# Feature parts kept once in DRAM and loaded in three runs, and the source row spread for plain quads alone

## The chip, the cores and the metric

The kernel runs on one core of a Trainium2 chip. The metric is the device time of one execution in microseconds; runs of the same kernel here lie within about 0.2% of each other (2110.19 to 2114.73 us for the kernel before). Engine names follow the profile: PE is TensorE's matmul, PEld its weight load, DVE is VectorE, ACT is ScalarE, POOL is GpSimd and SP is SyncE, which here only issues DMAs.

## The reference

One layer of a graph network with 6250 nodes, 128 features and 200,000 edges. The edges come sorted by `dst`; `src` is random.

```python
h   = maximum(layernorm(x), 0)
xw  = h @ W_in                                        # one row of 128 per node
W_e = (ssp(f_e @ W_f1 + b_f1) @ W_f2 + b_f2) * c_e    # f_e: 20 features of an edge, c_e: its weight
out = segment_sum(xw[dst_e] * W_e, src_e)             # gather by dst, add up by src
y   = x + ssp(out @ W_o1 + b_o1) @ W_o2 + b_o2        # ssp(v) = softplus(v) - log 2
```

## The kernel before, in words

**Units of work.** The edges are cut into chunks of 128, quads of 512 (four chunks; 391 of them) and super chunks of 1024 (two quads; 196). The main loop has one iteration per quad, and the order of every instruction is written out by hand: iteration `i` runs one stage of quad `i`, the next stage of quad `i-1`, and so on, and calls hooked functions at named points (`"L"`, `"D0"`, `"PE2"`, `"D2"`, ...). The order of recording is the order on each engine.

**What a quad passes through.** `s1_pe` (L290) multiplies the features by `W_f1` on PE; ACT computes Abs, Exp, Ln (L295 to L301); DVE adds up the softplus (L325). `s2_pe_x` (L340) picks the rows of `xw` by a one-hot matrix, `s2_pe_w` (L348) multiplies by `W_f2`, ACT scales (L353) and DVE multiplies (L358). What follows differs:

- A *plain* quad (237 of them) compares its sources with each other: `s1_eq` (L319) sets a row of 512 sources, spread over all 128 partitions in the tile `sb`, against the column of sources. `s3_pe` (L370) adds equal sources up, `s3_copy` (L378, ACT) copies the sums to the tile `s` (five buffers), `s3_ji` (L399, ACT) makes the row numbers, and `s3_scatter` issues four scatters (L418), one per chunk.
- A *permuted* quad (154 of them, list `mpq`: quads 8, 10, 13, 15, 18, ... to 390) is sorted by permutation matrices (L528, L621) into `accT` in SBUF. `s1_eq`, `s3_copy` and `s3_scatter` return at once for it, so it never reads `sb`. Two of them share one scatter of overflow rows: 77 in all.

**Scatters.** A scatter is an indirect DMA with add that POOL issues into one of four accumulators in DRAM. Two into the same accumulator may not overlap, so each waits for the one before it in its accumulator. `acc_of` picks the accumulator by the scatter's number `k`: 0 for the first two, then `k % 2` up to 8, `k % 3` up to 140 and `k % 4` after that. POOL's queue does almost nothing else from 48.8 us to 2048 us.

**Features.** A matmul in bf16 keeps fp32 accuracy here by splitting: `fb_1` to `fb_4` cut a block of 4096 edges' features into three bf16 parts (`f3[:, 0]`, `[:, 1]`, `[:, 2]`). The contraction has 6 x 20 = 120 rows, with the parts in the order 0, 0, 0, 1, 1, 2, and `ws` has the matching parts of `W_f1` (`part` in `_layout`: 0, 1, 2, 0, 1, 0). The order is laid out in DRAM: `fb_4` writes part 0 three times, part 1 twice and part 2 once into `fsd` (L260, L261, L262), and `load_sc` reads a super chunk's 120 rows in one DMA (L271).

**SP's queue.** For every super chunk `load_sc` issues `ft` (L271), `sb` (L273), two `rb` (L276) and, after loading four registers (L278), four `wn` (L283). `ft` has three static buffers and waits for PE's matmuls of three super chunks earlier; `sb` has three buffers and waits for the DVE comparison (L319) that last read its buffer. `load_sc(s)` stands at the start of iteration `2(s-2)`, ahead of that iteration's hooks. In the built program every DMA on SP also waits for the DMA eight before it on that queue. At the start SP runs, in this order: loads, the writes of block 0 to `fsd`, `load_sc(0)`, `load_sc(1)`, ten pieces that zero accumulator 1 (L148), `load_sc(2)` and so on.

**The end.** After the last quad the accumulators are read back, added, and sent through the output layers (L1076 to L1139).

Of the kernel before, what the change touches and what calls it, by code (L numbers as in the profile page):

```python
# [8 lines left out]
BF16 = mybir.dt.bfloat16  # L9
# [11 lines left out]
P = 128  # L21
SC = 1024
SEG = 512
# [16 lines left out]
HB = 64  # L40
NR = 3 * WIN
NACC = 4
CQ = 16
EARLY_N = 256

# [2 lines left out]
def tile_gnn(ctx: ExitStack, tc: tile.TileContext, x, fB, cT, srcT, srcr, dstr, win_, wf1, wf2, bias, bo1c, wo1,  # L48
             wo2, consts, ident, out, n_edges):
    nc = tc.nc  # L50
    N = out.shape[0]
    NP = x.shape[0]
    NB, RB, BE = fB.shape
    EP = NB * BE
    KF = 6 * RB
    K1 = KF + 3
    FE = RB * BE // P
# [17 lines left out]
    mpi = {q: n for n, q in enumerate(mpq)}  # L75
# [12 lines left out]
    dp = ctx.enter_context(tc.tile_pool(name="dp", bufs=1, space=DRAM))  # L88
# [6 lines left out]
    accs = []  # L95
    for k in range(NACC):
        a_ = dp.tile([ACC_R, P], F32, name=f"acc{k}")
# [1 line left out]
    tab = dp.tile([NP * 3, P], BF16, name="tab")  # L99
    reld = dp.tile([NSC, SC], BF16, name="reld")  # L100
    src16 = dp.tile([NSC, SC], I16, name="src16")
    fsd = dp.tile([NB, 6, RB * BE], BF16, name="fsd")
    dropd = dp.tile([P, EP // P], BF16, name="dropd")

    con = cp.tile([P, 16], F32, name="con")
# [150 lines left out]
    def fb_4(b):  # L256
        f3 = fst[b]["f3"]
        nc.vector.tensor_tensor(f3[:, 2], fst[b]["fr"], f3[:, 1], op=ALU.subtract)
        v = fsd[b].rearrange("g (p e) -> p g e", p=P)
        nc.sync.dma_start(v[:, 0:3], f3[:, 0:1].to_broadcast([P, 3, FE]))  # L260
        nc.sync.dma_start(v[:, 3:5], f3[:, 1:2].to_broadcast([P, 2, FE]))  # L261
        nc.sync.dma_start(v[:, 5:6], f3[:, 2:3])  # L262
        del fst[b]

    def load_sc(s):
        n = min(SC, NQ * SEG - s * SC)
        pp, hh, nh = s % HALF, s // HALF, n // SEG
        top = caps[s]
        ft = fts[s % len(fts)]
        b, o = s * SC // BE, s * SC % BE  # L270
        nc.sync.dma_start(ft[:KF, :n], fsd[b].rearrange("g (r e) -> (g r) e", r=RB)[:, o:o + n])  # L271
        sb = ld.tile([P, SC], I16, tag="sb", name="sb")
        nc.sync.dma_start(sb[:, :n], src16[s:s + 1, :n].to_broadcast([P, n]))  # L273
        rb = ld.tile([P, SEG], BF16, tag="rb", name="rb")
        for j in range(nh):
            nc.sync.dma_start(rb[j * HB:(j + 1) * HB], reld[s:s + 1, j * SEG:(j + 1) * SEG].to_broadcast([HB, SEG]))  # L276
        wn = ld.tile([P, 2, P], BF16, tag="wn", name="wn")
        _, regs = nc.values_load_multi_w_load_instructions(  # L278
            base_i[pp:pp + 1, hh, 0:2 * nh], engines=[SP], min_val=0, max_val=top,
            skip_runtime_bounds_check_because="clamped on the chip to [0, top]")  # L280
        for k in range(2 * nh):
            j, c = divmod(k, 2)
            nc.sync.dma_start(wn[j * HB:j * HB + NR, c, :], tab[bass.ds(regs[k] * 3, NR), :])  # L283
        loads[s] = (ft, sb, rb, wn)
# [65 lines left out]
    def s2_copy(q):  # L350
        xc = wk.tile([P, 4, P], F32, tag="xc", name="xc")
        for c in range(4):
            nc.scalar.mul(xc[:, c, :], st[q]["xg"][:, c, :], late["c", q // CQ][:, 4 * (q % CQ) + c:4 * (q % CQ) + c + 1])  # L353
        st[q]["xc"] = xc
# [297 lines left out]
    def c_load(b):  # L652
        n = min(4 * CQ, EP // P - 4 * CQ * b)
        t_ = ld.tile([P, 4 * CQ], F32, tag="cb", name="cb", bufs=2)
        nc.sync.dma_start(t_[:, :n], cT[:, 4 * CQ * b:4 * CQ * b + n])
        late["c", b] = t_
# [14 lines left out]
    with tc.manual_schedule():  # L671
# [98 lines left out]
        if NQ > 2:  # L770
            load_sc(1)
# [7 lines left out]
        def at(i, point, fn, *a):  # L779
            hooks.setdefault((i, point), []).append((fn, a))  # L780
# [11 lines left out]

        for b in range(1, -(-NQ // CQ)):
            at(CQ * b - CQ // 2, "L", c_load, b)

# [212 lines left out]
    with tc.For_i(0, trips, 1) as ci:  # L1008
        dcol = wk.tile([P, 1], I32, bufs=1, tag="dcol", name="dcol")
        nc.sync.dma_start(dcol, dstr.rearrange("s (e o) -> (s e) o", o=1)[bass.ds(ci * P, P), :])  # L1010
        rcol = wk.tile([P, 1], BF16, bufs=1, tag="rcol", name="rcol")
        nc.sync.dma_start(rcol, reld.rearrange("s (e o) -> (s e) o", o=1)[bass.ds(ci * P, P), :])
        scol = wk.tile([P, 1], I32, bufs=1, tag="scol", name="scol")
        nc.sync.dma_start(scol, srcr.rearrange("s (e o) -> (s e) o", o=1)[bass.ds(ci * P, P), :])
        ccol = wk.tile([P, 1], F32, bufs=1, tag="ccol", name="ccol")
        nc.sync.dma_start(ccol, cT[:, bass.ds(ci, 1)])
        xcol = wk.tile([P, 1], BF16, bufs=1, tag="xcol", name="xcol")
        nc.sync.dma_start(xcol, dropd[:, bass.ds(ci, 1)])
        sb = wk.tile([P, P], I32, bufs=1, tag="oeq", name="fsb")
        nc.sync.dma_start(sb, srcr.rearrange("s e -> (s e)")[bass.ds(ci * P, P)].unsqueeze(0).to_broadcast([P, P]))  # L1020
        ft = wk.tile([P, P], BF16, tag="oh", name="fft")
        nc.vector.memset(ft[96:P, :], 1.0)
        fsel = fsd.rearrange("b g (r e) -> b (g r) e", r=RB)
        nc.sync.dma_start(ft[:KF, :], fsel[bass.ds(ci // (BE // P), 1), :, bass.ds((ci % (BE // P)) * P, P)]
                          .rearrange("o m e -> (o m) e"))
        x3 = wk.tile([P, 3, P], BF16, tag="pt", name="fx3")
        nc.gpsimd.indirect_dma_start(out=x3.rearrange("p k f -> p (k f)"), out_offset=None,
                                     in_=tab.rearrange("(n k) f -> n (k f)", k=3),
                                     in_offset=bass.IndirectOffsetOnAxis(ap=dcol[:, 0:1], axis=0))
        ok = wk.tile([P, 4], F32, bufs=1, tag="ok", name="ok")  # L1030
        nc.vector.tensor_scalar(ok[:, 0:1], rcol, float(WIN), None, op0=ALU.is_ge)
        nc.vector.tensor_scalar(ok[:, 1:2], rcol, 0.0, None, op0=ALU.is_lt)
        nc.vector.tensor_tensor(ok[:, 2:3], ok[:, 0:1], ok[:, 1:2], op=ALU.add)
        nc.vector.scalar_tensor_tensor(ok[:, 3:4], ok[:, 2:3], xcol, ccol, op0=ALU.max, op1=ALU.mult)
        xw = wk.tile([P, P], F32, bufs=1, tag="rm", name="fxw")
        nc.vector.tensor_tensor(xw, x3[:, 0], x3[:, 1], op=ALU.add)
        nc.vector.tensor_tensor(xw, xw, x3[:, 2], op=ALU.add)
        z = ps.tile([P, P], F32, tag="A", name="fz", bufs=4)
        nc.tensor.matmul(z, ws, ft[:K1, :], start=True, stop=True)
        e = wk.tile([P, P], F32, tag="e", name="fe")  # L1040
        nc.scalar.activation(e, z, AF.Abs)
        nc.scalar.activation(e, e, AF.Exp, scale=-1.0)
        nc.scalar.activation(e, e, AF.Ln, bias=half, scale=0.5)
        a = wk.tile([P, P], F32, tag="a", name="fa")
        nc.vector.scalar_tensor_tensor(a, z, 0.0, e, op0=ALU.max, op1=ALU.add)
        W = ps.tile([P, P], F32, tag="A", name="fW", bufs=4)
        nc.tensor.matmul(W, onesb[HB:], b2rep[HB:, 0, :], start=True, stop=False)
        nc.tensor.matmul(W, a, w2, start=False, stop=True)
        m = wk.tile([P, 132], F32, tag="xc", name="fm")
        nc.vector.tensor_copy(m[:, 128:129], wgt)  # L1050
        nc.vector.scalar_tensor_tensor(m[:, :P], W, ok[:, 3:4], xw, op0=ALU.mult, op1=ALU.mult)
        eq = wk.tile([P, P], F32, tag="eq", name="feq")
        nc.vector.tensor_tensor(eq, sb, scol.to_broadcast([P, P]), op=ALU.is_equal)
        pp = ps.tile([P, 132], F32, tag="B", name="fpp", bufs=4)
        nc.tensor.matmul(pp[:, :129], eq, m[:, :129], start=True, stop=True)
        s = wk.tile([P, P], F32, bufs=1, tag="dg", name="fs")
        nc.scalar.copy(s, pp[:, :P])
        dlt = wk.tile([P, 2], F32, bufs=1, tag="dlt", name="dlt")
        nc.vector.tensor_scalar(dlt[:, 0:1], scol, trash, None, op0=ALU.subtract)
        nc.vector.scalar_tensor_tensor(dlt[:, 1:2], pp[:, 128:129], wgt2, dlt[:, 0:1], op0=ALU.is_lt, op1=ALU.mult)  # L1060
        ji = wk.tile([P, 1], I32, bufs=1, tag="fji", name="fji")
        nc.vector.tensor_scalar(ji, dlt[:, 1:2], trash, None, op0=ALU.add)
        nc.gpsimd.indirect_dma_start(out=accs[1][:, :], out_offset=bass.IndirectOffsetOnAxis(ap=ji[:, 0:1], axis=0),
                                     in_=s, in_offset=None, compute_op=ALU.add)
# [172 lines left out]
def _layout(inputs):  # L1237
    import numpy as np

    p = "L0_gnn_"  # L1240
# [3 lines left out]
    n, e = x.shape[0], src.shape[0]  # L1244
# [19 lines left out]
    con[:, 14] = np_ // GRP // 2 - con[:, 3]  # L1264
    con[:n_sc // 2, 5] = caps[:n_sc // 2]
    con[:n_sc // 2, 6] = caps[n_sc // 2:]
    part = np.array([0, 1, 2, 0, 1, 0])
    for r in range(6 * rb + 3):
        con[r, 7 + (part[r // rb] if r < 6 * rb else r - 6 * rb)] = 1.0
    for r in range(3):  # L1270
# [39 lines left out]
```

## Time and profile before

| what | value |
|---|---|
| runs shown | 2110.86 us median of 3 (2110.19 to 2114.73) |
| the profiled execution's own time | 2108.97 us |
| its span, first to last instruction | 2107.2 us |
| granted TensorE clock, mean | 0.976 |
| DMA issues of `ft`, `sb`, `fsd` | 196 of up to 240 KB; 196 of up to 256 KB; 49 each of 480, 320 and 160 KB |
| issue time on SP, median: L271 / L273 / L260 | 382 / 354 / 416 ns |
| plain scatters, L418 | 948; 1532 / 1542 / 2782 ns (min / median / max) |

The page gives busy time by engine, and the span in 40 slices. Groups of instructions are read as "line, engine, operation, output <- input, count | busy, mean of one | idle time before, and what ended it". In the view of waits a row is "who <- what it waited for: us in total, times, longest". In a timeline a row is "start, duration, engine, line", and the bracket at its end is the idle time before it and what ended that.

### The profile page before, as it was taken

The page shows a single profiled execution, that of the slowest core. Times are in us where ns is not written, and L with a number is a line of the kernel's source. Part 1 is how long each engine was busy: PE and PEld are TensorE (multiplying, and loading weights), DVE is VectorE, ACT ScalarE, POOL GpSimd, SP SyncE. Part 2 cuts the span into 40 slices and gives each one's busy share as a digit, 9 for nine tenths or more (in the row PEclk, how much of TensorE's full clock was granted, in tenths as well). Part 3 has the DMA queues.
Part 4 walks back from the last instruction along what each step waited for, and adds up shares of the span by engine and source line. Part 5 has one row for each costly group of instructions (what it writes and reads, how often), then busy time and mean ns, then how long its engine had stood idle before and what let it go on. Part 6 is the DMA issues. An engine that isn't in the chain of part 4 may idle for free. (4 is left out here: it accounts for less than half of the span.)

```text
span 2107.2 us, 56868 instructions
## 1 busy us (share of the span) xinstructions
PE 1926.4 (91%) x19917; PEld 1402.2 (67%) x19917; DVE 1774.3 (84%) x4749; ACT 1793.4 (85%) x4789; POOL 1685.2 (80%) x1067
## 2 busy tenths in 40 slices
PE   3788999999999999999999999999999999999976
PEld 2566666676767666766666677777777766766644
DVE  4767888888889898888888989898988988888855
ACT  4687988898989898988889999989899889988824
POOL 2677878888888888888887888888888888888874
PEclk9888999999999999999999999999999999999997
DMA  7986767777777777777776777777777777777739
GB/s 266 237 179 126 153 133 144 135 155 137 152 136 154 141 140 147 152 141 141 152 142 140 144 140 135 152 140 150 137 152 149 142 138 143 138 132 161 138 39 240
DMA packets 394833, 314.79 MB, mean 149 GB/s; under 512 B 94863, under 2 KB 334266, under 8 KB 394546
## 3 DMA queue, kind: packets, MB, share of 16 engines
q1 hardware_dynamic: 245858, 240.57, 39.4%
q0 software_dynamic: 148400, 70.52, 34.8%
q8 instruction: 156, 2.56, 0.5%
q14 instruction: 131, 1.07, 0.2%
q10 hardware_dynamic: 288, 0.07, 0.0%
HBM read 173.32 MB, written 137.67 MB: 148 GB/s over the span
## 5 line engine op out<-in xcount | busy, mean ns | idle before, releaser
L418 POOL DMA_INDIRECT acc<-s,ji x948 | 1523.7, 1607 | 348.1 <-issue 225.6
L528 PE MATMUL pq<-pt,pm 128*128 128x387 bf16 x2464 | 487.0, 337 | 32.9 <-ACT s L378 18.7
L353 ACT ACTIVATE xc<-xg,cb 128x128 f32<-128x128 f32 x1564 | 446.5, 374 | 64.7 <-PE xg L340 50.1
L348 PE MATMUL W<-w,a 128*128 128x128 f32 x3128 | 462.5, 292 | 0.0
L348 PEld LDWEIGHTS W<-w,a 128*128 128x128 f32 x3128 | 386.9, 195 | 41.7 <-issue 2.0
L621 PE MATMUL un<-so,mst 32*128 32x392 bf16 x7392 | 359.4, 329 | 35.1 <-DVE pr L468 14.8
L528 PEld LDWEIGHTS <-pm 128*128 128x128 bf16 x2464 | 241.2, 98 | 195.3 <-issue 40.3
L621 PEld LDWEIGHTS <-mst 32*128 32x128 bf16 x7392 | 227.1, 94 | 162.3 <-issue 63.4
L325 DVE SCALAR_TENSOR_TENSOR a<-z,e 128x512 f32<-128x512 f32 x391 | 266.9, 683 | 64.9 <-ACT e L301 37.1
L301 ACT ACTIVATE e<-e,con 128x512 f32<-128x512 f32 x391 | 282.3, 722 | 12.7
L370 PEld LDWEIGHTS pp<-m,eq 128*128 128x128 f32 x1896 | 254.5, 196 | 32.6 <-DVE accT L632 13.7
L370 PE MATMUL pp<-m,eq 128*128 128x129 f32 x1896 | 260.8, 281 | 12.4 <-DVE accT L632 9.0
L534 ACT CAST mst<-pq 128x387 bf16<-128x387 f32 x616 | 264.2, 481 | 6.2 <-PE pq L528 4.7
L295 ACT ACTIVATE e<-z 128x512 f32<-128x512 f32 x391 | 241.7, 618 | 18.5 <-PE z L290 17.8
L296 ACT ACTIVATE e<-e 128x512 f32<-128x512 f32 x391 | 246.5, 630 | 12.4
L378 ACT COPY s<-pp 128x258 f32<-128x258 f32 x474 | 165.2, 391 | 91.2 <-DMA acc<-s,ji 34.4
L358 DVE TENSOR_TENSOR m<-W,xc 128x512 f32<-128x512 f32 x237 | 162.3, 685 | 69.7 <-ACT xc L353 49.6
L518 DVE TENSOR_TENSOR pt<-pt 128x512 f32<-128x512 f32 x308 | 212.5, 690 | 0.0
L504 DVE TENSOR_SCALAR pm<-iot,pos 128x576 bf16<-128x576 f16 x616 | 202.0, 389 | 0.0
L358 DVE TENSOR_TENSOR pt<-W,xc 128x512 f32<-128x512 f32 x154 | 105.9, 687 | 81.2 <-ACT xc L353 50.5
L632 DVE TENSOR_TENSOR accT<-un,accT 128x392 f32<-128x392 f32 x288 | 142.8, 557 | 36.9 <-PE un L621 26.2
L290 PE MATMUL z<-ft,ws 123*128 123x512 bf16 x391 | 152.2, 390 | 18.3 <-DMA ft<-fsd 18.3
(156 smaller groups left out, 2710.6 us busy)
## 6 DMA issues: line engine op xcount, KB each, us to landing
sb<-src SPq DMA_DIRECT2D x195, 256.0 KB
ft<-fsd SPq DMA_DIRECT2D x195, 240.0 KB
rb<-reld SPq DMA_DIRECT2D x391, 64.0 KB
fsd<-f SPq DMA_DIRECT2D x49, 480.0 KB
fb<-in_fB_dram SPq DMA_DIRECT2D x49, 320.0 KB
fsd<-f SPq DMA_DIRECT2D x49, 320.0 KB
acc<-s,ji POOLq DMA_INDIRECT x948
wn<-tab SPq DMA_DIRECT2D x782, 15.8 KB
```

Of the source, the lines that this page charges most:

```text
L295: nc.scalar.activation(e, st[q]["z"], AF.Abs)
L296: nc.scalar.activation(e, e, AF.Exp, scale=-1.0)
L301: nc.scalar.activation(e, e, AF.Ln, bias=half, scale=0.5)
L325: nc.vector.scalar_tensor_tensor(a, st[q]["z"], 0.0, st[q]["l"], op0=ALU.max, op1=ALU.add)
L348: nc.tensor.matmul(W[:, c, :], st[q]["a"][:, c * P:(c + 1) * P], w2, start=False, stop=(c == 3))
L353: nc.scalar.mul(xc[:, c, :], st[q]["xg"][:, c, :], late["c", q // CQ][:, 4 * (q % CQ) + c:4 * (q % CQ) + c + 1])
L358: nc.vector.tensor_tensor(m[:, :, :P], st[q]["W"], st[q]["xc"], op=ALU.mult)
L370: nc.tensor.matmul(pp[:, c, :129], st[q]["eq"][:, k, :], m[:, k, :129], start=True, stop=True)
L418: nc.gpsimd.indirect_dma_start(out=accs[k][:, :], out_offset=bass.IndirectOffsetOnAxis(ap=ji, axis=0), in_=s, in_offset=None, compute_op=A ...
L528: nc.tensor.matmul(t[:, :PW], mp[q]["pm"][:, c, s * P:(s + 1) * P], high(mp[q]["pt"][:, c:c + 1, :PW])[:, 0], start=(c == 0), stop=(c == 3))
L534: nc.scalar.copy(mp[q]["ms", s][:, :PW], mp[q].pop(("q", s))[:, :PW])
L621: nc.tensor.matmul(ts[g][:, :GN], mp[q]["ms", s][v, k * P:(k + 1) * P], mp[q]["oh"][v], start=(q == qs[0] and k == 0), stop=(q == qs[-1] a ...
```

## The change

`fsd` holds each block's three parts once (three runs of 20 rows instead of six), written by one DMA. `load_sc` reads the 120 rows of `ft` in three DMAs: 60 rows (parts 0, 1, 2), 40 rows (parts 0, 1) and 20 rows (part 0). So the rows' parts now stand as 0, 1, 2, 0, 1, 0, and the weights' as 0, 0, 0, 1, 1, 2; the six products are the same. The row of sources is spread into `sb` only for the plain quads of the super chunk: 42 super chunks have two of them, 153 have one and the last has none. The loop for edges that the main path can't take, which runs zero times on these inputs, is changed alike. Lines after L43 move down by a few in the changed file; `fb_4`'s write is L260 there, the load of `ft` L270 and the load of `sb` L276.

```diff
+FPARTS = ((0, 3), (3, 2), (5, 1))
...
-    fsd = dp.tile([NB, 6, RB * BE], BF16, name="fsd")
+    fsd = dp.tile([NB, 3, RB * BE], BF16, name="fsd")
...
-        v = fsd[b].rearrange("g (p e) -> p g e", p=P)
-        nc.sync.dma_start(v[:, 0:3], f3[:, 0:1].to_broadcast([P, 3, FE]))
-        nc.sync.dma_start(v[:, 3:5], f3[:, 1:2].to_broadcast([P, 2, FE]))
-        nc.sync.dma_start(v[:, 5:6], f3[:, 2:3])
+        nc.sync.dma_start(fsd[b].rearrange("g (p e) -> p g e", p=P), f3)
...
-        nc.sync.dma_start(ft[:KF, :n], fsd[b].rearrange("g (r e) -> (g r) e", r=RB)[:, o:o + n])
+        for g, m in FPARTS:
+            nc.sync.dma_start(ft[g * RB:(g + m) * RB, :n],
+                              fsd[b, :m].rearrange("g (r e) -> (g r) e", r=RB)[:, o:o + n])
         sb = ld.tile([P, SC], I16, tag="sb", name="sb")
-        nc.sync.dma_start(sb[:, :n], src16[s:s + 1, :n].to_broadcast([P, n]))
+        own = [j for j in range(nh) if 2 * s + j not in mpi]
+        if own:
+            v = slice(own[0] * SEG, (own[-1] + 1) * SEG)
+            nc.sync.dma_start(sb[:, v], src16[s:s + 1, v].to_broadcast([P, len(own) * SEG]))
...
-    part = np.array([0, 1, 2, 0, 1, 0])
+    part = np.array([0, 0, 0, 1, 1, 2])
```

More of the change, by code (lines that the diff above doesn't have):

```diff
@@ L1023, in tile_gnn @@
         fsel = fsd.rearrange("b g (r e) -> b (g r) e", r=RB)
-        nc.sync.dma_start(ft[:KF, :], fsel[bass.ds(ci // (BE // P), 1), :, bass.ds((ci % (BE // P)) * P, P)]
-                          .rearrange("o m e -> (o m) e"))
+        for g, m in FPARTS:
+            nc.sync.dma_start(ft[g * RB:(g + m) * RB, :], fsel[bass.ds(ci // (BE // P), 1), :m * RB,
+                                                               bass.ds((ci % (BE // P)) * P, P)]
+                              .rearrange("o m e -> (o m) e"))
         x3 = wk.tile([P, 3, P], BF16, tag="pt", name="fx3")
```

## The prediction

> **What bounds the kernel now.** I read the page's shares first. No engine is full over the span, so the page alone doesn't name the bound.
>
> ```profile
> PE 1926.4 (91%) x19917; PEld 1402.2 (67%) x19917; DVE 1774.3 (84%) x4749; ACT 1793.4 (85%) x4789; POOL 1685.2 (80%) x1067
> ```
>
> Then POOL's timeline in the middle, because the costliest group of the page is its scatter (L418: 948 of 1607 ns on average):
>
> ```profile
> 1003.77 1.54 POOL L418 DMA_INDIRECT acc<-s,ji  x1 [0.30 <-issue]
> 1005.62 1.54 POOL L418 DMA_INDIRECT acc<-s,ji  x1 [0.30 <-issue]
> 1007.47 1.54 POOL L418 DMA_INDIRECT acc<-s,ji  x1 [0.30 <-ACT mst L534]
> ```
>
> The scatters stand back to back: 1.54 us, then 0.30 us whatever the named releaser. So POOL's "80%" is a full queue, and 1025 scatters (948 + 77) of 1.61 + 0.30 = 1.91 us make 1958 us of the 2107. POOL runs so from 48.82 us (first scatter) to 2048.67 (end of the last); before lies the start, behind it 58.5 us of tail. Next, POOL's waits from 62 to 352 us:
>
> ```profile
> POOL acc L418 <- issue: 31.6, 92, 3.4
> POOL acc L418 <- DMA acc<-s,ji: 18.2, 20, 2.5
> ...
> POOL acc L418 <- ACT e L296: 4.3, 5, 1.9
> ```
>
> All its rows in this stretch sum to 68.1 us before 134 scatters. At 0.305 each, 40.9 is the fixed part and 27.2 us is extra; between 352 and 1040 the extra is nil. 4.5 of it is the third scatter, which belongs to the start. The other **22.7 us** fall where the scatters use two or three accumulators, so that each waits for the landing of the one two or three before. Single waits show it:
>
> ```profile
> 96.91 1.54 POOL L418 DMA_INDIRECT acc<-s,ji  x1 [1.61 <-DMA acc<-s,ji]
> 99.49 1.54 POOL L418 DMA_INDIRECT acc<-s,ji  x1 [1.03 <-DMA acc<-s,ji]
> ```
>
> The first was held until 7.27 us after the scatter three before it had started; three scatters without extra take 5.54. On SP's timeline `fsd` is issued at 89.51, 90.05 and 90.64, `ft` at 91.84, `sb` at 93.12: the slow landings stand in a burst of just the transfers that the change cuts. Of the 12 extra waits between 130 and 352 us, 6 come within 10 us of an `fsd` write, which stands there once in some 42 us, so that a quarter would by chance.
>
> Is the rest ready for a faster POOL? I set the end of each quad's `ji` on ACT (L399) beside its first scatter. Data is ready some 20 us ahead from 120 to 500 us, 12 at 614, 6 at 918, 0.3 at 1126, and 20 again from 1655. So up to 500 us POOL holds the others back, through the five `s` buffers; from 500 to 1126 PE, ACT and DVE lose ground, but POOL waits for them only some 3 us around 1126; from there POOL is the pace. ACT's waits of 62 to 352 us show the first hold:
>
> ```profile
> ACT s L378 <- DMA acc<-s,ji: 23.9, 9, 5.5
> ```
>
> So an earlier POOL before 352 us lets ACT move up too, by 23.9 us at most, and the gain reaches the end.
>
> **The change, part by part.**
>
> *Bytes removed.* `fsd`: 49 x 480 KB less. `sb`: 154 spreads of 128 KB less (153 super chunks with one plain quad, one with none has 128 KB). That is 24.1 + 20.2 = 44.3 MB of 314.79. SP's queue moves 240.57 MB for 39.4% of the 16 DMA engines, so some 7 points of the mean 74% go. In a burst of block write, `ft` and `sb` 960 + 240 + 256 KB become 480 + 240 + 128, 42% less; in the bursts without a write 496 KB become 368, 26% less.
>
> *What that is worth.* In the steady state nothing directly: no engine waits for a load between 52 us and the tail, and POOL has no extra waits. In the 22.7 us, something. A landing that comes at 7.0 us must come at 5.5 to hold nobody, and its excess follows the queue ahead of it. If all of the excess went with the bytes, 26 to 42% would go, and since only what exceeds 5.54 us counts, more than that; if the rest of the queue (the zeroing of accumulators until 123 us, the scatters' own 70.52 MB) makes it, little goes. Bounds 0 and -22.7; I take a third, **-7.5 us**. The same kind of extra from 1900 to 2050 us, after the switch back to three accumulators, is 2.3 us: **-0.8**.
>
> *The ft load in three.* 392 issues more on SP, 98 fewer for `fsd`, one fewer for `sb`: at their medians 392 x 0.38 - 98 x 0.41 = 109 us more work for SP. The queue has room: it idles 467 us in front of `sb`, and the new issues stand ahead of that wait.
>
> ```profile
> SPq L273 <- DVE eq L319: 466.9, 113, 9.7
> ```
>
> Behind it stand `rb` and `wn`, and from super chunk 10 on at least 12 us lie between the issue of `ft`, `rb` or `wn` and its first reader. The tightest reader is DVE's statistics of x, 4.3 us behind its load at worst; one or two late ones may cost 1 us. Cost in the steady state 0; without the cover it would be the 109 us.
>
> *PE's wait for three semaphores.* The weight load ahead of L290 now waits for three landings instead of one, which adds a semaphore instruction of 51 ns (the row of L340 has 63 such) for each of 196 super chunks, at most 10 us. In the trace these run while PE still has three or four queued matmuls: one at 544.554 us stands amid the eight loads of L348, whose 0.11 us steps don't change. So 0; upper bound 5.3, the 104 before 1126 us, where PE sets the pace.
>
> *The start.* Here there is no cover. SP issues without a break from 25.4 to 63 us, and the first scatter (48.82) follows from `z` at 45.15, which waited 6.58 us for `ft` of super chunk 2.
>
> ```profile
> 25.39 1.23 SPq L271 DMA_DIRECT2D ft<-fsd  x1
> ...
> 40.35 0.90 SPq L271 DMA_DIRECT2D ft<-fsd  x1
> ```
>
> Two issues more at super chunk 0 are hidden: between its `ft` (18.47 + 0.35) and `sb` (20.44) SP waited 1.6 us. Of the four at super chunks 1 and 2, each costs between 0 (the queue is full and only bytes count; the ten zero pieces go at 0.76 us for 320 KB) and 1.23 us: 0 to +4.9. I take 0.35 for two and 0.3 for the others, **+1.3**. The next two scatters (55.37 and 62.12) each wait for the landing of the one before; nothing but block 0's early write gets smaller until then, so 0, bounds -1.5 and +1.5.
>
> *The scatter itself.* Its mean is 65 ns over its median: 62 us. Those that overlap L518 on DVE are 0.15 us long beyond 1.54, the others 0.04, so I put this down to work on DVE, which stays: 0, bound -6 (a tenth, the share of DMA time that goes).
>
> **Sum.** 2108.97 (the profiled execution: span 2107.2 and 1.8 around it) + 1.3 - 7.5 - 0.8 = 2102.0. The median of the runs is 1.9 above that execution, so on its scale 2103.9: **2104 us, 0.3% faster**.
>
> **A rule against the change.** The Trainium skill, "DMA: Bandwidth & Descriptors", in "Why a DMA increments its semaphore by 16 and not by 1", says that a DMA from SP runs on the largest number of engines up to 16 that divides the outermost size. By that 120 rows go to 15 engines, 60 to 15, 40 and 20 to ten. The busiest engine would carry ten rows of `ft` instead of eight, so that `ft` with half an `sb` shrinks from 16 to 14 rows there, not by 26%; the gain would then come mostly from the block writes, and I would put -3.5 where I have -7.5. The trace of before doesn't tell engines apart. The same page, "Bandwidth", calls transfers under 64 KB mostly overhead, which would hit the 40 KB part; the rows here show the cost of an issue alone, 0.35 us.
>
> **Rivals.**
>
> 1. *No change to measure* (0.27). The excess landing time is not the queue's, or PE, ACT and DVE don't follow and POOL gives it back at 1126 us. Then -0.8 to -2 against +1.3: 2110 us. For it: most scatters between 130 and 352 us land in time under the same 74%.
> 2. *Slower* (0.18). The split at the start: SP is the last there, so three super chunks with two issues of 1.23 us each push the first scatter by 7.4 us, and the queue behind it keeps the landings slow: 2118. It decides if the first scatter starts after about 61 us with the gain of 8.3 intact, or after 53 with no gain. Against it: from 35 to 40 us the DMA share is 1.03, so bytes rule there.
> 3. *All of it goes* (0.08): -22.7 - 2.3 + 1.3: 2087.
>
> **Numbers.** Forecast 0.47 (2097 to 2106.5), rivals 0.27, 0.18, 0.08. 0.2%, about what can be told from no change here, is 4.2 us. Faster takes in the forecast and rival 3, 0.55; same 0.27; slower 0.18. For 8 in 10 I leave out most of rival 3 and the worse half of rival 2: 2091 to 2115.
>
> **What would show it.** Right: L418's extra waits from 62 to 352 us fall to about 15 us and ACT's for `s` with them; the first scatter stands at 50 us; scatters at 1000 us are still 1.54 + 0.30; DMA share near 67%; no waits for `ft` on PE after 52 us. Wrong: `z` waiting for `ft` in the middle of the span, a first scatter past 53 us, or POOL waiting for ACT by tens of us around 1126.

## The result, and the profile after

The changed kernel takes 2103.46 us (median of 13 runs, 2099.07 to 2110.22), the kernel before 2115.66 us in the runs that alternate with them (median of 13, 2109.29 to 2121.47). The ratio is **0.9952 [0.9939, 0.9966]**: 0.48% faster, about 10 us. The same kernel differs by more than the 0.2% of the three runs shown first: single runs of the kernel before spread by 0.6% here, and its median differs by up to 12 us between chips and sessions (2106.96, 2107.47 and 2103.54 below). So only ratios to the kernel before in the same session are compared.

The page's busy times, in the same columns as those of before. No engine's work changed by more than 4 us:

```profile
PE 1923.0 (91%) x19917; PEld 1400.2 (67%) x19917; DVE 1770.9 (84%) x4749; ACT 1792.5 (85%) x4789; POOL 1687.1 (80%) x1067
```

The page's row of all DMA traffic, and its rows of SP's queue (q1) and of POOL's (q0), with packets, MB and the share of the 16 DMA engines:

```profile
DMA packets 378228, 270.57 MB, mean 129 GB/s; under 512 B 97199, under 2 KB 337242, under 8 KB 377938
...
q0 software_dynamic: 148400, 70.52, 36.1%
q1 hardware_dynamic: 229250, 196.31, 33.7%
```

Of 314.79 MB, 44.2 are gone, and SP's queue fell from 39.4% to 33.7%. The scatters' own queue moves the same 70.52 MB, and its packets take 36.1% for 34.8% before.

POOL's timeline around 1004 us shows the steady state unchanged, 1.54 us and then 0.30 whatever the releaser:

```profile
1004.07 1.54 POOL L421 DMA_INDIRECT acc<-s,ji  x1 [0.30 <-issue]
1005.92 1.54 POOL L421 DMA_INDIRECT acc<-s,ji  x1 [0.31 <-issue]
1007.77 1.54 POOL L421 DMA_INDIRECT acc<-s,ji  x1 [0.30 <-ACT s L381]
```

POOL's waits from 62 to 352 us, the four largest rows (what it waited for: us in total, times, longest):

```profile
POOL acc L421 <- issue: 29.6, 96, 0.6
POOL acc L421 <- DMA acc<-s,ji: 16.2, 17, 2.5
POOL acc L421 <- DMA acc<-accT: 6.0, 2, 4.0
POOL acc L421 <- ACT e L298: 5.9, 5, 1.6
```

All rows of this view sum to 65.9 us before 143 scatters. Less 143 x 0.305 that is 22.3 us extra; 3.7 of it is the third scatter's, which belongs to the start, and 18.6 us remain. The prediction's 22.7 us for before came from its nine largest rows alone (68.1 us before 134 scatters); all its rows sum to 70.6 us before 139, which leaves 23.7. The name of a releaser matters little here: waits named after ACT are extra waits too if they last over 0.30 us.

The same stretch of the timeline that showed before's slow landings, a burst with a block write (`fsd` is issued at 92.25 us now):

```profile
92.78 1.59 POOL L421 DMA_INDIRECT acc<-s,ji  x1 [0.30 <-issue]
94.67 1.62 POOL L421 DMA_INDIRECT acc<-s,ji  x1 [0.30 <-issue]
96.60 1.54 POOL L421 DMA_INDIRECT acc<-s,ji  x1 [0.30 <-issue]
98.92 1.54 POOL L421 DMA_INDIRECT acc<-s,ji  x1 [0.78 <-DMA acc<-s,ji]
```

The scatter at 98.92 started 6.14 us after the one three before it (92.78). In before the worst of this burst had 7.27. Two extra waits of 1.31 and 0.73 us have become one of 0.48.

ACT's waits for a free `s` buffer, 62 to 352 us, follow:

```profile
ACT s L381 <- issue: 8.3, 4, 6.1
...
ACT s L381 <- DMA acc<-s,ji: 6.1, 5, 2.9
```

Before had 23.9 us under the second name and none under the first: 14.4 us now. (The view names no releaser for the hold of 6.1 us; in before the copy at the same place, 115.57 us, waited 5.50 us for a landing, so it is counted here.)

### The profile page after: what moved, and what is told of

It is laid out like the page before. It is cut to its first block, busy times and chain, and to the rows that moved or that the text cites. A ratio compares the mean times of both kernels' runs of the same rounds, so it can differ in the third digit from the quotient of the medians.

```text
span 2101.6 us, 57225 instructions
## 1 busy us (share of the span) xinstructions
PE 1923.0 (91%) x19917; PEld 1400.2 (67%) x19917; DVE 1770.9 (84%) x4749; ACT 1792.5 (85%) x4789; POOL 1687.1 (80%) x1067
## 3 DMA queue, kind: packets, MB, share of 16 engines
q0 software_dynamic: 148400, 70.52, 36.1%
q1 hardware_dynamic: 229250, 196.31, 33.7%
## 5 line engine op out<-in xcount | busy, mean ns | idle before, releaser
L304 ACT ACTIVATE e<-e,con 128x512 f32<-128x512 f32 x391 | 282.4, 722 | 12.7
L361 DVE TENSOR_TENSOR pt<-W,xc 128x512 f32<-128x512 f32 x154 | 106.0, 688 | 82.4 <-ACT xc L356 48.8
L293 PE MATMUL z<-ft,ws 123*128 123x512 bf16 x391 | 152.3, 390 | 17.3 <-DMA ft<-fsd 8.7
```

Source lines behind the costliest of these rows:

```text
L361: nc.vector.tensor_tensor(m[:, :, :P], st[q]["W"], st[q]["xc"], op=ALU.mult)
```

## The experiments

The theory: the removed bytes make the scatters' landings earlier, which is worth something only in the stretch where two or three accumulators are in use (to scatter 140, about 350 us), and what POOL gains there reaches the end. The rivals: bytes count evenly over the whole span; or a gain of POOL is handed back later, because PE, ACT and DVE don't follow. Beside these stands the cost of the split load at the start.

Each result is the ratio to the kernel before, run in turn with it on the same chip, with its 95% interval; e1 to e4 share one chip, e5 to e8 a second and e9 to e12 a third. "Extra" is, as above, POOL's waits before scatters beyond 0.305 us each, now counted by the scatter's number `k` (the first is 0) and from the timeline of the one profiled execution.

**e1, the features alone.** The changed kernel with the whole row of sources spread for every super chunk, as before:

```diff
-        own = [j for j in range(nh) if 2 * s + j not in mpi]
-        if own: ...
+        nc.sync.dma_start(sb[:, :n], src16[s:s + 1, :n].to_broadcast([P, n]))
```

> The features alone: parts written once, ft in three loads, sb spread in full as before. Theory L (landings: fewer bytes ahead of a scatter in the DMA engines let it land sooner while the scatters use two or three accumulators, up to scatter 140 at about 350 us): the block writes are the larger half of each burst, so about -5 us of the -10 that the whole change gave, with the first scatter 2.3 us late as in the whole change. Rival W (work everywhere: less DMA traffic speeds the whole span evenly, by bytes): 24.1 of 44.3 MB, also about -5, but spread over the span, so that scatter 140 is only 1 us earlier. Rival S (the narrower sb is all of the gain, and the three loads cost): +2.

Measured 2102.82 us, 0.9977 [0.9958, 0.9996]. Scatter 140 starts 3.4 us earlier than in before (348.2 us against 351.6), where an even spread over the span would give 1 us.

**e2, the spread alone.** The kernel before, with only the row of sources spread for plain quads:

```diff
-        nc.sync.dma_start(sb[:, :n], src16[s:s + 1, :n].to_broadcast([P, n]))
+        own = [j for j in range(nh) if 2 * s + j not in mpi]
+        if own:
+            v = slice(own[0] * SEG, (own[-1] + 1) * SEG)
+            nc.sync.dma_start(sb[:, v], src16[s:s + 1, v].to_broadcast([P, len(own) * SEG]))
```

> The spread of sources for plain quads alone; features as before (six copies, one load). Theory L: 20.2 MB less and no late start, about -5 us, first scatter at 48.8 us, scatter 140 some 5 us earlier. Rival W: about -5, spread evenly over the span. Rival S: -12.

Measured 2103.63 us, 0.9981 [0.9964, 0.9997]. Scatter 140 starts 6.2 us earlier, as the theory had it. This is the one run in which bytes alone are removed.

**e3, the split alone.** The kernel before, with six copies in DRAM as ever, but `ft` loaded in three DMAs. No byte is saved:

```diff
-        nc.sync.dma_start(ft[:KF, :n], fsd[b].rearrange("g (r e) -> (g r) e", r=RB)[:, o:o + n])
+        for g, m in FPARTS:
+            nc.sync.dma_start(ft[g * RB:(g + m) * RB, :n],
+                              fsd[b, g:g + m].rearrange("g (r e) -> (g r) e", r=RB)[:, o:o + n])
```

> The kernel before with ft read in three loads of 60, 40 and 20 rows from the six copies: no byte saved. Theory L: the start cost alone, first scatter some 2 us later and the total +2 us (0 to +4). Rival S: the split lengthens landings as well (ten rows of ft on the busiest engine), +6 us or more and more extra waits of the scatters before 350 us.

Measured 2102.73 us, 0.9980 [0.9961, 0.9998], which no theory had. The first scatter is late as expected (50.3 us against 48.8), yet the whole is a little faster; the longer landings and the +6 us of the rival S did not come. So the split is at least no loss; that it is a gain is weakly shown (the interval ends at 0.9998). Beside it e1, which takes 24 MB away on top of the split, gains no more. The three intervals overlap so widely that the 0.48% can't be divided among the parts, and a share of it may be the split's and not the bytes'.

**e4 and e5, four accumulators from scatter 36 on**, in the kernel before and in the changed one, so that landings have 7.4 us instead of 5.5:

```diff
-    K1_END, K2_END, K3_END = 2, 8, 140
+    K1_END, K2_END, K3_END = 2, 8, 36
```

> The kernel before with the fourth accumulator used from scatter 36 instead of 140, so that a scatter from about 139 us on may land 7.4 us after its start without holding the next. Theory L: the 12 us of extra waits from 130 to 352 us nearly go, about -10 us, and the data's lead over POOL still suffices. Rival W: the waits are not what the bytes shorten, but this takes them away too; it would also be about -10. Rival H (PE, ACT and DVE can't follow; POOL gives all back around 1126 us): 0.

> The changed kernel with the fourth accumulator from scatter 36. Theory L: the 8 us of extra waits that the changed kernel keeps from 130 to 352 us go too; about -16 us against the kernel before, some 6 below the changed kernel. Beside the same step made in the kernel before, the change then gives about -5 where it gave -10, since the waits it shortened are gone. Rival W: the two add up, -20.

Measured 2115.58 us, 1.0044 [1.0022, 1.0066], and 2111.47 us, 1.0018 [1.0008, 1.0028]. The edit did something else as well. The last pieces that zero accumulator 3 are issued in iterations up to 23, after the first scatters into it in these kernels; they also erase what those scatters had added, so by the order of the program a part of the sums is lost in e4, e5 and e8. SP's waits of e4 from 62 to 250 us show the price:

```profile
SPq L148 <- DMA acc<-s,ji: 31.4, 2, 29.7
```

SP stands for up to 29.7 us before a zeroing piece, for the landing of a scatter, and everything behind it on that queue is late. Scatter 140 starts 12 us earlier than before (339.5 against 351.6), but then 15 us of gaps on POOL between scatters 140 and 500 wait for late data. These runs say nothing of landings; e10 and e11 repeat them without the fault.

**e6 and e7, the change in time.** e6 makes the change for the first 18 blocks and 72 super chunks alone (`b < 18`, `s < 72`; the last of these `ft` is issued at 753 us, not at the 370 us that the expectation names) and e7 for the rest. Both have the changed row order; the unchanged part writes six copies and loads them in one DMA:

```diff
-        nc.sync.dma_start(fsd[b].rearrange("g (p e) -> p g e", p=P), f3)
+        v = fsd[b].rearrange("g (p e) -> p g e", p=P)
+        nc.sync.dma_start(v[:, 0:3], f3)
+        if not b < 18:
+            nc.sync.dma_start(v[:, 3:5], f3[:, 0:2])
+            nc.sync.dma_start(v[:, 5:6], f3[:, 0:1])
...
-        own = [j for j in range(nh) if 2 * s + j not in mpi]
+        own = [j for j in range(nh) if 2 * s + j not in mpi or not (s < 72)]
```

> The change for blocks 0 to 17 and super chunks 0 to 71 alone (up to about 370 us); after that six copies, one ft load and a full sb, with the rows in the changed kernel's order throughout. Theory L: all of the gain but 1 us, -9. Rival W: 72 of 196 super chunks, -4.

> The change for blocks from 18 and super chunks from 72 on alone. Theory L: -1 (the extra waits after 1900 us), first scatter at 48.8 us. Rival W: -6.

Measured 2102.42 us, 0.9979 [0.9965, 0.9994], and 2109.91 us, 1.0011 [1.0001, 1.0021]. e7 takes 28.2 of the 44.2 MB away and gains nothing: bytes do not count evenly over the span. What gains is the early part, though less than the whole change.

**e8, the two together**, four accumulators from scatter 36 with the change for all blocks but block 0, which is written and loaded as before (the edit for `b` as in e6, with `b > 0`, and that of e4):

> The changed kernel with the fourth accumulator from scatter 36, and block 0 kept as before (six copies, one ft load for super chunks 0 to 3), so that the start is not late. Theory L: 2 us below the changed kernel with four accumulators, -18 against the kernel before, first scatter at 48.8 us. Rival W: no better than that kernel, since the saved bytes of block 0 are back.

Measured 2109.39 us, 1.0010 [0.9993, 1.0027], with the fault of e4.

**e9, the changed kernel again**, beside the following three:

> The changed kernel once more, beside the next three on one chip, since the parts alone came to 0.2% each and the kernel before moved by 0.4% between chips. Theory L: 0.5% below the kernel before again. Rival P (a part of the first difference was the chips' own): 0.2 to 0.3%, as much as the parts alone.

Measured 2094.60 us, 0.9953 [0.9935, 0.9970], as before. Its profile is a second execution of the changed kernel. POOL's waits from 62 to 352 us, first two rows:

```profile
POOL acc L421 <- issue: 29.2, 95, 0.4
POOL acc L421 <- DMA acc<-s,ji: 14.7, 20, 2.0
```

By the same working (61.2 us before 145 scatters, less the third's 3.9) 13.1 us are extra here, against 18.6 in the first execution: one execution gives this sum to some 6 us only.

**e10, four accumulators from scatter 64 on, in the kernel before.** By then all of accumulator 3 is zeroed in the order of the program:

```diff
-    K1_END, K2_END, K3_END = 2, 8, 140
+    K1_END, K2_END, K3_END = 2, 8, 64
```

> The kernel before with the fourth accumulator from scatter 64, the first that is recorded after the last zeroing piece, so that SP waits for no scatter. Theory L: of the extra waits before scatters 64 to 139 (7.1 us in the profile of before) nearly all go; scatter 140 some 6 us earlier, total -6 us. Rival H (the others can't follow and POOL gives it back by 1126 us): scatter 140 earlier, scatter 540 not, total 0.

Measured 2105.04 us, 1.0005 [0.9988, 1.0021]. The extra waits of scatters 64 to 140 fell from 7.1 to 2.7 us, and scatter 140 starts 6.0 us earlier than in before. At scatter 540 only 1.0 us is left of it. POOL's waits of e10 from 352 to 1130 us, and after them those of the kernel before:

```profile
POOL acc L418 <- ACT ji L399: 8.3, 10, 3.8
```

```profile
POOL acc L418 <- ACT ji L399: 3.9, 4, 2.0
```

The row numbers (`ji`) of a quad now come late ten times instead of four. ACT finishes them for quad 56 at 355.5 us, in before at 355.1: POOL had moved forward and the others had not. This is the rival that hands the gain back.

**e11, the same in the changed kernel**, with block 0 written and loaded as before (e8 with 64 in place of 36):

> The changed kernel with block 0 as before (six copies, one ft load for super chunks 0 to 3) and the fourth accumulator from scatter 64. Theory L: first scatter at 49 us instead of 51, extra waits of scatters 64 to 139 near 0; 6 to 8 us below the changed kernel. Rival H: scatter 140 earlier, the end not, same as the changed kernel.

Measured 2093.72 us, 0.9947 [0.9925, 0.9968], not to be told from e9's 0.9953. Its first scatter stands at 48.7 us, that of before, so the cost at the start is that of block 0's split load and can be had back; a gain in the time is not to be seen.

**e12, more bytes.** The kernel before with one more DMA for each block, which writes part 0 six times (960 KB) to a DRAM tensor that nobody reads:

```diff
+    fsx = dp.tile([NB, 6, RB * BE], BF16, name="fsx")
...
+        nc.sync.dma_start(fsx[b].rearrange("g (p e) -> p g e", p=P), f3[:, 0:1].to_broadcast([P, 6, FE]))
```

> The kernel before with one DMA more per block, which writes part 0 six times (960 KB) to a DRAM tensor that nobody reads: 47 MB more, twice what the change takes from the block writes, in 49 issues. Theory L: the extra waits of the scatters before scatter 140 grow from 24 us by some 8 to 12, first scatter at 49 us, total +6 to +12 us. Rival N (the bytes in the queue don't set the landings): extra waits 24 us, total 0 to +1.

Measured 2142.28 us, 1.0177 [1.0142, 1.0211]: +37 us for 48 MB. The page's row of the traffic, POOL's waits from 62 to 352 us and those from 352 to 1130 us:

```profile
DMA packets 433251, 362.98 MB, mean 170 GB/s; under 512 B 95647, under 2 KB 372682, under 8 KB 432962
```

```profile
POOL acc L420 <- DMA acc<-s,ji: 33.1, 26, 4.3
```

```profile
POOL acc L420 <- DMA acc<-s,ji: 14.8, 26, 2.3
```

From 352 to 1130 us before had:

```profile
POOL acc L418 <- DMA acc<-s,ji: 4.9, 16, 0.3
```

The first of e12's two waits was 18.2 us in before; the extra waits up to scatter 140 rose from 23.8 to 34.5. The second was these 4.9 us in 16 times, which is 16 x 0.305: with four accumulators landings held nobody in before, and now they do (14.8 less 26 x 0.305 is 6.9 us). Over all scatters past 140 the extra waits that bear the name of a landing sum to 21 us, for 1.6 in before. So more bytes do make the landings later, and the stretch where that matters grows with them.

**The landings themselves.** The traces also have the records, up to 16 for each scatter, that its DMA makes on its semaphore; the last of them before the semaphore's next use is taken as the landing. The mean time from a scatter's start to its landing, in us, for scatters that start between 62 and 740 us and between 820 and 1890 us (e6 and e7 change over between the two), with the number over 5.54 us, the time of three scatters (3 x 1.847):

| kernel | 62 to 740 | over 5.54 | 820 to 1890 | over 5.54 |
|---|---|---|---|---|
| e10, bytes as before | 4.37 | 48 of 341 | 4.23 | 43 of 558 |
| e7, changed late | 4.41 | 55 of 338 | 4.06 | 26 of 559 |
| e6, changed early | 4.19 | 32 of 343 | 4.31 | 69 of 559 |
| changed, e9 | 4.16 | 26 of 346 | 4.07 | 31 of 560 |
| e12, more bytes | 4.66 | 75 of 333 | 4.53 | 92 of 552 |

So the change makes landings some 0.2 us earlier on average wherever it is made, and e7 has this too and gains nothing by it: there no scatter was waiting. The traces of before, the changed kernel and e1 to e4 hold only some 10 of these 16 records, so they are compared among themselves alone. (A scatter counts here with 8 records or more.) From 820 to 1890 us their means are 3.97 (before) and 4.03 (e4, same bytes), 3.89 (e1), 3.90 (e2), 3.89 (e3) and 3.86 (changed). The split at equal bytes (e3) seems to move the landings about as far as either saving of bytes.

**All runs side by side.** Times of scatters in us; extra waits in us by the scatter's number; "POOL" is the change of the third scatter's start plus the change of all extra waits, against before; "measured" is (ratio - 1) x 2111 us.

| kernel | first scatter | third | extra, 3 to 140 | extra, 141 to 1024 | POOL | measured |
|---|---|---|---|---|---|---|
| before | 48.8 | 62.1 | 23.8 | 5.8 | | |
| changed | 51.1 | 63.2 | 18.7 | 1.2 | -8.6 | -10.1 |
| changed, e9 | 50.2 | 63.3 | 11.8 | 6.9 | -9.7 | -9.9 |
| e1 features | 51.9 | 65.6 | 19.0 | 5.9 | -1.2 | -4.9 |
| e2 spread | 49.5 | 64.1 | 16.7 | 7.7 | -3.2 | -4.0 |
| e3 split | 50.3 | 62.4 | 21.4 | 3.3 | -4.6 | -4.2 |
| e6 early | 49.9 | 62.3 | 20.1 | 6.2 | -3.1 | -4.4 |
| e7 late | 49.5 | 63.2 | 25.7 | 1.6 | -1.2 | +2.3 |
| e10 64 | 49.3 | 61.8 | 19.9 | 11.6 | +1.6 | +1.1 |
| e11 changed, 64 | 48.7 | 62.4 | 12.7 | 7.6 | -9.0 | -11.2 |
| e12 more bytes | 49.5 | 63.1 | 34.5 | 33.1 | +39.0 | +37.4 |

POOL's waits and its start account for every measured change to within 4 us. That says much for e12 and for the whole change, and little for e1, e2, e3, e6, e7 and e10, whose changes are 1 to 5 us themselves; each row is one execution, and the row of before is from another session than e1 to e12. What an execution adds to this by chance is the scatters' own length: their time beyond 1.542 us each sums to 57 to 70 us, without order among the kernels.

## Why the prediction was right, and where it was not

**Direction and size.** 0.3% faster was forecast, 0.48% measured. The profiled execution was put at 2102.0 us; the changed kernel's took 2103.46. That the times agree so closely is luck: the median of all 13 runs of the kernel before is 4.8 us above that of the three runs the forecast started from, and the gain was 10 us where 7 were forecast. Where the time comes off was no luck: it is in waits of POOL for the landings of its own scatters.

**Landings up to scatter 140, forecast -7.5.** 23.8 us became 18.7 and 11.8, so -5.1 and -12.0 in two executions. That bytes do this is seen in e2, where bytes alone are removed (weakly by itself: the interval ends at 0.9997), and clearly in e12, with the opposite sign and more bytes. e7 shows that earlier landings late in the span are worth nothing. That bytes alone do it in the whole change is not shown, because the split (e3) may have a share. The DMA share, which was to fall to near 67%, is 70.5% by the queues' rows, for 74.9% before. The late term, forecast -0.8 (after the switch back to three accumulators): 2.4 us became 1.2 and 0.5.

**The start, forecast +1.3.** The first scatter moved by +2.3 and +1.4. The three issues of `ft` on SP, with time and duration:

```profile
18.39 1.12 SPq L270 DMA_DIRECT2D ft<-fsd  x3
...
25.71 3.13 SPq L270 DMA_DIRECT2D ft<-fsd  x3
...
41.49 2.08 SPq L270 DMA_DIRECT2D ft<-fsd  x3
```

At super chunk 1 three issues take 3.13 us for 1.23 of the single one, at super chunk 2 they take 2.08 for 0.90. That is 1.9 and 1.2 us, within the 0 to 4.9 that was given and above the 1.3 that was taken. At the third scatter 1.1 and 1.2 us of the delay are left. The rival that the start makes it slower did not come: the scatter would have had to stand past 53 us.

**PE's wait for three semaphores, forecast 0.** In the view of line L293 the semaphore instruction stands there 196 times at 51 ns:

```profile
L293 PEldq EVENT_SEMAPHORE  x196: 51/51/51, 21.9 to 1992.7; - x196
```

After 52 us PE has no wait for `ft`, as was said, and none before this line at all: the last of its six waits there ends at 47.5 us. So the time is covered.

**SP's room, forecast 0.** The idle time before `sb` fell from 466.9 us to 337.7, and the work took it:

```profile
SPq L276 <- DVE eq L322: 337.7, 89, 8.9
SPq L260 <- DVE f L259: 187.1, 40, 10.1
```

There is still idle time in front of `sb`, so the queue keeps up.

**The step that failed.** "So an earlier POOL before 352 us lets ACT move up too, by 23.9 us at most, and the gain reaches the end." That holds for the first part of the stretch, not up to 352 us. e10 takes 4.4 us of waits from scatters 64 to 140 (196 to 350 us) and of the 6.0 us by which scatter 140 is early, 1.0 is left at scatter 540. From quad 56 on (`ji` at 355 us) PE, ACT and DVE run at one pace in all kernels, to within some 2 us: quad 229 has `ji` ready at 1237.7 us in before, 1226.7 and 1226.5 in the changed kernel, 1228.1 in e11, 1235.9 in e10, 1248.9 in e12. At quad 56 the difference to before was already -8.7 and -9.5 us for the changed kernel and +0.4 for e10; it was -3.4, -6.2, -2.4, -6.0 and +0.9 for e1, e2, e3, e6 and e7, which lies within 3 us of what each of these runs measured. So what is to reach the end must be won by the others as well, before about quad 56. (In e12 it was +11.2; the rest of its 37 us comes later, from the landings themselves.) The 20 us of data that are ready ahead, which the prediction read as POOL holding the rest back, were a reserve, which in before is used up by 1126 us.

**What holds the others early.** ACT can't copy sums while all five `s` buffers are waiting for a landing, and PE stands behind ACT. In before such a hold lies ahead of the copy at 180.66 us, the waiting time and its releaser in the bracket; PE's next matmul, at 181.09 us, had waited 6.60 us for that copy:

```profile
180.66 0.65 ACT L378 COPY s<-pp 128x258 f32<-128x258 f32 x2 [5.41 <-DMA acc<-s,ji]
```

The windows of 10 us around it, before and then in the changed kernel (window, length, busy us of PE, PEld, DVE, ACT, POOL with counts, granted TensorE clock, DMA share, GB/s):

```profile
170.00:180.00 10.00, 4.06 (x37) 3.62 (x36) 7.24 (x25) 5.16 (x16) 7.48 (x5) 0.84 0.77 147
180.00:190.00 10.00, 8.91 (x50) 5.71 (x51) 4.81 (x12) 7.64 (x18) 7.93 (x5) 0.65 0.38 48
```

```profile
170.00:180.00 10.00, 8.69 (x71) 6.41 (x72) 9.72 (x32) 9.25 (x26) 8.08 (x6) 1.00 0.76 140
180.00:190.00 10.00, 9.17 (x75) 7.03 (x76) 6.79 (x18) 8.87 (x26) 8.47 (x6) 1.00 0.82 161
```

PE does 87 matmuls in these 20 us of before and 146 in the changed kernel. Part of that is the hold itself, part the clock, which is at 0.65 in the window after it: 50 matmuls fill 8.91 us there, and 75 fill 9.17 us at 1.00. The same eight matmuls of `s2_pe_w` take 2.08 us at 184.94 us in before and 1.16 at 184.25 in the changed kernel. The prediction counted the hold and not the clock. ACT's holds for `s` from 62 to 352 us sum to 23.9 us in before, 14.4 and 7.8 in the changed kernel, 22.2 in e10.

**What stays open.** How the gain divides between the bytes and the split. e3 saves no byte and is not a loss, perhaps a gain, and its landings seem earlier too; e1 beside it does not show that the feature bytes are worth anything more. One reading is that with three smaller DMAs in a queue where each waits for the one eight before it, fewer bytes are under way at once, but that is argued, not tried. Early (0.9979) and late (1.0011) do not add up to 0.9953, by some 8 us. To scatter 140 e6 and the changed kernel run the same transfers, and their scatter 140 differs by 3 to 8 us in single executions on different chips, so this may be variation between executions or chips; it is not settled. No version was found that is faster than the change: e11 is not to be told from it.

## What to carry to other kernels

Here removing bytes paid only in the stage where something waits for a transfer's landing; find that stage first (here 60 to 350 us, two or three accumulators), and expect little from the same bytes elsewhere (e7). Where a change cuts bytes and also splits a transfer, run the split alone (e3): it may be a part of the gain. Before counting a wait on the pacing queue as won, look at which engine is next late and whether it moves too: a reserve of finished data ahead of the queue shrinks first (e10). And a buffer can't be brought into use earlier than the program's order clears it; else the queue that clears it waits for its users (e4).

## What the runs showed of the hardware

- The granted TensorE clock fell with a hold and stayed low after it. In before it is 0.50 from 176.8 to 187.1 us, for a hold of ACT of 5.41 us that ends at 180.66, and 1.00 in the changed kernel in the same stretch, without the hold. Around the hold near 115 us, which both kernels have, it is 0.86 from 102 to 152 us in both. After the hold of 5.41 us the same eight matmuls took 2.08 us for 1.16, so there the stall cost more than its own length.
- The price of DMA traffic on scatters that wait for each other was not linear here: 44 MB less gained 10 us, 48 MB more cost 37. The transfers are not of the same kind, but a reason is seen: of some 820 landings between scatters 141 and 960, 36 took over 7.39 us, the time of four scatters (4 x 1.847), in e12, 3 in e10 and none in e9.
- Three issues on SP's queue cost more than three medians (0.33 us each) where SP issues without a break: 3.13 us at 25.71 us, against 1.12 us for the same three at 18.39.
